# A small copy moved ahead of two others on ScalarE, and twenty unread products near the end

## The chip, the cores and the metric

The kernel runs on one core of a Trainium2 chip. A core has five engines that run side by side, each with a queue of instructions of its own: TensorE (PE in the profile, its weight loads PEld), VectorE (DVE), ScalarE (ACT), GpSimd (POOL) and SyncE (SP), which here only issues DMA transfers. TensorE writes its results to PSUM, which is divided into banks (a tile of 512 float32 numbers per partition fills one here); the other engines carry them from there to SBUF. The metric is the device time of one execution in microseconds. The time before is 2628.5 us, the median of three runs (2627.23 to 2629.38).

## The reference

Two cross-attention layers follow one another on 64 sequences of 256 positions and 320 channels (20 heads of 16). Each sequence has 77 context rows of 512. Cut to what is computed:

```
# layer 0 (the last four of 81 context rows would be image rows; with 77 there are none)
out_text = softmax(q k^T / 4) v              # per head, over 77 context rows
x = x + (out_text) Wo + bo

# layer 1: the first 73 rows are text, the last 4 are image tokens
probs_t  = softmax(q k_t^T / 4)              # over 73
text_out = probs_t v_t
qsem     = l2norm(probs_t text)              # 512 wide, per head and position
sem      = qsem . l2norm(image)^T            # 4 numbers
probs_ip = softmax(q k_ip^T / 4 + 0.5 sem) * spatial_mask
ip_out   = probs_ip v_ip
out      = x + (text_out + ip_out) W_out + b_out
```

All of it is float32.

## The kernel before, in words

x is kept transposed, channels on partitions. Sequences are worked on in pairs: 32 pairs, with index p. A pair has 10 units: two sequences (b), and five units (u) of each, where a unit is 128 positions by 8 heads (the last unit of five takes both halves of the positions for 4 heads). One loop, over g, does one step per unit of layer 0, and beside it one unit of layer 1 that lies 13 steps back. `k = g % 10` is the place of a step in its round of ten; k = 8 is the ninth step, and its successor k = 9 the tenth. After the 320 steps of layer 0 the loop goes on for 25 more, in which layer 1 ends.

A step issues this, in the order of the program:

1. TensorE writes one PSUM tile `sc` of four banks. First come the *semantics* of the layer-1 unit of two steps before (`before1`): its transposed weights times a stored matrix that holds, side by side, the products of the context rows with each other, the values, and ones (lines 755 and 761). Then come the scores of the unit of layer 0 and of the unit of layer 1 (line 641). There is one such tile (`bufs=1`), so these writes wait until all readers of the step before are done.
2. VectorE takes the maximum of the scores (659) and subtracts it (661), for each layer.
3. `transposed(1, ...)`: TensorE transposes the layer-1 weights of the step before (705, 706) and ScalarE copies them out (712, 713). These are read by the next step's 755 and 761.
4. ScalarE computes the exponential for layer 0 (669).
5. `weighted`: VectorE multiplies the first 73 columns of the semantics, in `sc`, by the weights (772, 775), for the norm of `qsem`.
6. `first`: other work of the pipeline, listed by `fillers(k, p)`. In the ninth step these are one or two chunks of value rows: TensorE products (379), and a ScalarE copy (380).
7. `transposed(0, ...)`: the layer-0 weights of the step before, on TensorE (705, 706) and ScalarE (731, 732; 720 and 723 for the fifth unit). Their readers are 788 and 793, in `attend`, after the second and the fifth unit of a sequence.
8. The sums copy (1114): ScalarE copies the other 21 columns of the semantics for 8 heads, 168 numbers per partition, from `sc` to SBUF: four similarities to image tokens, 16 sums of values and the sum of the weights. VectorE's products of point 5 and this copy read the same banks and are kept in order by a wait on VectorE.
9. ScalarE computes the exponentials for layer 1 (672, 673); GpSimd copies the image scores (676).
10. VectorE and GpSimd normalise layer 0 (687, 688, 692), VectorE reduces the products of point 5 (1125).
11. `second` and `third`: more of `fillers`. The last products with image weights (`image_attend_last`, 947) stand here in the ninth step, and the output projection of layer 1 (`project`, 528 and 537, then `project_last`, 616) begins in the tenth.

The order on TensorE, ScalarE, VectorE and GpSimd is the order of the program, held by `keep_order`. SyncE's DMA issues are ordered by a scheduler from the second round on, so an edit elsewhere can shift them.

In the steps after the 320, TensorE has less to do, and `keep_busy(n)` issues n products of the identity with itself into a tile that nobody reads (741). In the very last steps the path is: image weights transposed (914) and copied (916), image outputs (926), VectorE's addition of them (934), the last third of them (947, 951), the output projection (528, 537, 601, 616, 620) and the transfers out.

Of the kernel before, what the change touches and what calls it, by code (L numbers as in the profile page):

```python
# [21 lines left out]
TT = T - NIP  # L22
# [12 lines left out]
UNITS = ((0, 0), (0, 1), (1, 0), (1, 1), (2, 0))  # L35
# [3 lines left out]
NU = 2 * len(UNITS)  # L39
# [24 lines left out]
def tile_two_cross_attentions(ctx: ExitStack, tc: tile.TileContext, a: dict, out: bass.AP):  # L64
# [35 lines left out]
    nc = tc.nc  # L100
    x_in, c_in, cip_in = a["x"], a["ctx"], a["ctx_ip"]
    NB = x_in.shape[1] // S
    NP = NB // 2
# [104 lines left out]
    def load_more(g):  # L208
        queue = nc.sync
        if g == 1:  # L210
            queue.dma_start(cip, cip_in.rearrange("(k p) t -> p k t", p=P))
            load_ctx_weight("wkip1", queue, wkip)
        elif g == 3:
            load_ctx_weight("wvip1", queue, wvip)
        elif g == 5:
            wo[0], bo[0] = load_out("wo0", queue), load_bias("bo0", queue)
        elif g == 6:
            wq[1] = load_chan("wq1", queue)
        elif g == 8:
            wo[1], bo[1] = load_out("wo1", queue), load_bias("bo1", queue)  # L220
            queue.dma_start(smask, a["smask"])
# [404 lines left out]
    stats = {}  # L626
    ws, pts = {}, {}

    def eight(t, u):

        return t[:, PLACES[u] : PLACES[u] + 8].rearrange("p (r e) ... -> p r e ...", e=2)
# [14 lines left out]
    def shifted(ps, l, p, b, u):  # L646


        nt = (T, TT)[l]
        name = f"{l}_{p}_{b}{u}"  # L650
        if l and u == 0:
            stats[p, b] = (
                small.tile([P, 2 * H, NIP], F32, tag="att", name=f"att{p}_{b}", bufs=3),
                big.tile([P, 2 * H, NIP + D + 1], F32, tag="sums", name=f"sums{p}_{b}", bufs=3),
                small.tile([P, 2 * H], F32, tag="nrm", name=f"nrm{p}_{b}", bufs=3),
            )
        sc = ps[:, :, 2 * T * l : 2 * T * (l + 1)].rearrange("p r (e t) -> p r e t", t=T)
        mx = small.tile([P, 4, 2], F32, tag="mx", name=f"mx{name}")
        nc.vector.tensor_reduce(mx, sc[:, :, :, :nt], AX.X, ALU.max)  # L659
        w = ws[l] = sp.tile([P, 4, 2, T], F32, tag=f"w{l}", name=f"w{name}", bufs=2 - l)  # L660
        nc.vector.tensor_tensor(  # L661
            w, sc, mx.unsqueeze(3).broadcast_to([P, 4, 2, T]), ALU.subtract
        )

    def exponential(l, g, p, b, u):

        w = ws[l]
        if not l:
            nc.scalar.activation(w, w, AF.Exp, scale=SCALE)  # L669
            return  # L670
        two = ws[l] = parts1[g % 3]
        nc.scalar.activation(two[:, :4].rearrange("p (e a) j t -> p (a j) e t", e=2), w[:, :, :, :M], AF.Exp, scale=SCALE)  # L672
        nc.scalar.activation(  # L673
            rests(two), w[:, :, :, M:TT], AF.Exp, scale=SCALE
        )
        nc.gpsimd.tensor_copy(eight(stats[p, b][0], u), w[:, :, :, TT:])  # L676

    def rests(two):

        r = two[:, 4].rearrange("p j (a c) -> p (j a) c", c=QR)  # L680
        return r[:, :, : 2 * R1].rearrange("p r (e t) -> p r e t", e=2)
# [52 lines left out]
    def keep_busy(n):  # L734


        if n:
            ps = ptr.tile([P, 4, P], F32, tag="tr", name=f"busy{len(busy)}")
            busy.append(n)
            for i in range(n):  # L740
                nc.tensor.transpose(ps[:, i % 4, :], ident, ident)
# [24 lines left out]
    def by_block(ps):  # L766
        return ps[:, :, SEM0 : SEM0 + 2 * GV].rearrange("p r (e t) -> p r e t", t=GV)

    def weighted(ps, p, b, u, w):
        sm = by_block(ps)  # L770
        prod = sp.tile([P, 4, 2, TT], F32, tag="prod", name=f"prod{p}_{b}{u}", bufs=1)
        nc.vector.tensor_tensor(  # L772
            prod[:, :, :, :M], sm[:, :, :, :M], w[:, :4].rearrange("p (e a) j t -> p (a j) e t", e=2), ALU.mult
        )
        nc.vector.tensor_tensor(prod[:, :, :, M:], sm[:, :, :, M:TT], rests(w), ALU.mult)  # L775
        return prod
# [40 lines left out]
    def text_output(p, b):  # L817

        sums = stats[p, b][1]
        rec = small.tile([P, 2 * H], F32, tag="rec", name=f"rec{p}_{b}", bufs=2)  # L820
        nc.vector.reciprocal(rec, sums[:, :, NIP + D])
        an = big.tile([P, 2, H, D], F32, tag="an", name=f"an{p}_{b}", bufs=1)
        by_head(an, sums[:, :, NIP : NIP + D], rec)
        return an
# [36 lines left out]
    def image_least(p, b):  # L861


        total = stats[p, b][1][:, :, NIP + D]
        t = least[p, b] = small.tile([P, 2 * H], F32, tag="least", name=f"least{p}_{b}", bufs=1)
        nc.gpsimd.tensor_mul(t, total, total)

    def image_squares(p, b):
        r = stats[p, b][2]
        nc.vector.scalar_tensor_tensor(r, least[p, b], EPS * EPS, r, ALU.mult, ALU.max)  # L870
# [181 lines left out]
    def unit(g):  # L1052
        return (g // NU, g % NU // len(UNITS), g % len(UNITS)) if 0 <= g < NP * NU else None
# [6 lines left out]
    for fn in held.pop("q")():  # L1060
        fn()

    last0 = last1 = before1 = None
    later, early = {}, {}
    for g in range(NP * NU + LAG + 12):
        p, k = divmod(g, NU)
        first, second, third, begin = fillers(k, p)
        if g == NU + 3:
            in_order = len(nc.cur_bb.bb.instructions)
        load_more(g)  # L1070
        now = [unit(g), unit(g - LAG)]
        ps = prod = None
        for fn, args in early.pop(g, ()):
            fn(*args)
        drains = [fn for what in ("q", "o") if what in held for fn in held.pop(what)()]
        if now[0] or now[1] or before1:
            ps = psc.tile([P, 4, 512], F32, tag="sc", name=f"sc{g}")
            todo = []
            if before1:
                todo.append((semantics, (*before1[:3], before1[4])))  # L1080
            for l in range(2):
                if now[l]:
                    todo.append((scores, (l, *now[l])))
            for n, (fn, args) in enumerate(todo):
                fn(ps, n == 0, n == len(todo) - 1, *args)
        for fn, args in begin:
            fn(*args)
        if "i" in held:
            drains += held.pop("i")()
        for fn in drains:  # L1090
            fn()
        for l in range(2):
            if now[l]:
                shifted(ps, l, *now[l])
        new1 = None
        if last1:
            transposed(1, *last1)
            new1 = (*last1, pts[1])
        if now[0] and k != 5:
            exponential(0, g, *now[0])  # L1100
        if before1:
            prod = weighted(ps, *before1[:4])
        for fn, args in first:
            fn(*args)
        if last0:
            transposed(0, *last0)
        idle = g - NP * NU
        if idle > 2:
            keep_busy(14 if now[1] else {13: 12, 14: 16, 15: 14, 16: 16, 17: 16}.get(idle, 0))
        if now[0] and k == 5:  # L1110
            exponential(0, g, *now[0])
        ends = before1 and before1[2] == len(UNITS) - 1
        if before1:
            nc.scalar.copy(eight(stats[before1[:2]][1], before1[2]), by_block(ps)[:, :, :, TT:])  # L1114
            if ends:
                image_least(*before1[:2])
        if now[1]:
            exponential(1, g, *now[1])
        for fn, args in later.pop(g, ()):
            fn(*args)  # L1120
        if now[0]:
            normalize(g)
        if before1:
            q, b, u = before1[:3]
            nc.vector.tensor_reduce(eight(stats[q, b][2], u), prod, AX.X, ALU.add)  # L1125
            if ends:
                image_squares(q, b)
                made["an"] = text_output(q, b)
                later[g + 1] = [(image_scores, (q, b))]
                early[g + 2] = [(image_shifted, (q, b)), (image_exponential, (q, b))]  # L1130
                early[g + 3] = [(image_weights, (q, b))]
        for fn, args in second:
            fn(*args)
        if last0:
            q, b, u, _ = last0
            if u == 1 or u == len(UNITS) - 1:
                attend(q, b, int(u > 1))
        for fn, args in third:
            fn(*args)
        if ends:  # L1140
            image_norm(*before1[:2])
        last0 = (*now[0], ws[0]) if now[0] else None
        before1 = new1
        last1 = (*now[1], ws[1]) if now[1] else None
# [51 lines left out]
```

## Time and profile before

| | |
|---|---|
| Median of three runs | 2628.5 us (2627.23 to 2629.38) |
| The profiled execution's own time | 2627.7 us |
| Its span, first to last instruction | 2626.0 us |
| Mean granted TensorE clock | 0.996 |
| Sums copy, line 1114 | 320 times, 302 ns each |
| VectorE's wait that ends the idle time before it | 119.0 us (189 times) |
| Copy of transposes, line 731 | 256 times, 588 ns each |
| Unread products, line 741 | 214 records, 2536.3 to 2607.7 us |

The profile is of one execution. A group row gives source line, engine, operation, the tile written and those read, the count; then busy time in us and mean ns of one; then the engine's idle time just before these instructions and what ended it. A row of the timeline or the chain has start, duration, engine and line. In a row for a stretch of time, the granted clock (1.00 is full speed) stands after the busy times, and then the share of the DMA engines and their GB/s. L705 is line 705.

### The profile page before, as it was taken

The page shows a single profiled execution, that of the slowest core. Times are in us where ns is not written, and L with a number is a line of the kernel's source. Part 1 is how long each engine was busy: PE and PEld are TensorE (multiplying, and loading weights), DVE is VectorE, ACT ScalarE, POOL GpSimd, SP SyncE. Part 2 cuts the span into 40 slices and gives each one's busy share as a digit, 9 for nine tenths or more (in the row PEclk, how much of TensorE's full clock was granted, in tenths as well). Part 3 has the DMA queues.
Part 4 walks back from the last instruction along what each step waited for, and adds up shares of the span by engine and source line. Part 5 has one row for each costly group of instructions (what it writes and reads, how often), then busy time and mean ns, then how long its engine had stood idle before and what let it go on. Part 6 is the DMA issues. An engine that isn't in the chain of part 4 may idle for free.

```text
span 2626.0 us, 74027 instructions
## 1 busy us (share of the span) xinstructions
PE 2558.2 (97%) x27006; PEld 1981.0 (75%) x27006; DVE 1972.3 (75%) x3641; ACT 1539.2 (59%) x3989; POOL 1440.1 (55%) x3514
## 2 busy tenths in 40 slices
PE   7999999999999999999999999999999999999998
PEld 5677777777777777777777777777777777777676
DVE  3577777777777777777777777777777777777764
ACT  3465665665665665665665665665665665665553
POOL 2455555565555566555566555566555556555542
PEclk9999999999999999999999999999999999999999
DMA  5212211112111112211112111112211112211000
GB/s 163 72 29 58 58 42 47 42 51 57 51 50 47 43 51 56 58 43 47 42 52 57 51 50 47 42 52 57 56 46 47 42 52 56 55 41 36 26 22 23
DMA packets 154657, 132.26 MB, mean 50 GB/s; under 512 B 48248, under 2 KB 132984, under 8 KB 154296
## 3 DMA queue, kind: packets, MB, share of 16 engines
q1 hardware_dynamic: 153432, 126.38, 17.9%
q8 instruction: 216, 3.54, 0.6%
q14 instruction: 145, 1.19, 0.2%
q10 hardware_dynamic: 864, 1.15, 0.1%
HBM read 89.53 MB, written 33.91 MB: 47 GB/s over the span
## 4 chain that ended last, share of the span: by engine, by line
PE 85%; DVE 7%; ACT 3%; DMA 2%; issue 1%; POOL 1%; SPq 1%; DVEq 0%; POOLq 0%; ACTq 0%
PE sc L755 12%; PE tr L705 11%; PE o_ps L528 8%; PE sc L641 7%; PE v_ps L379 6%; PE sc L761 4%; PE q_ps L528 4%; PE q_ps L555 4%; PE k_ps L334 4%; PE o_ps L616 3%; PE o_ps L537 3%; PE pv L788 2%; DVE w L661 2%; PE q_ps L563 2%; PE q_ps L557 2%; DVE mx L659 2%
## 5 line engine op out<-in xcount | busy, mean ns | idle before, releaser
L659 DVE TENSOR_REDUCE mx<-sc 128x8 f32<-128x584 f32 (+1 forms) x640 | 497.8, 778 | 461.1 <-PE sc L641 461.1
L692 POOL TENSOR_TENSOR parts<-w,sm 128x512 f32<-128x512 f32 (+1 forms) x640 | 439.7, 708 | 299.8 <-ACT parts L673 180.7
L661 DVE TENSOR_TENSOR w<-sc,mx 128x616 f32<-128x616 f32 x640 | 512.0, 800 | 66.7 <-DVE mx L659 0.5
L712 ACT COPY pt<-tr 128x512 f32<-128x512 f32 x320 | 186.8, 584 | 446.6 <-PE tr L705 435.0
L705 PE MATMUL tr<-ident,parts 128*128 128x128 f32 x2560 | 410.4, 283 | 11.1 <-POOL parts L692 5.3
L755 PEld LDWEIGHTS sc<-gv,pt 64*128 64x128 f32 x5120 | 317.9, 188 | 108.8 <-ACT sums L1114 60.3
L755 PE MATMUL sc<-gv,pt 64*128 64x94 f32 x5120 | 357.6, 279 | 27.9 <-ACT sums L1114 27.7
L705 PEld LDWEIGHTS tr<-ident,parts 128*128 128x128 f32 x2560 | 283.0, 141 | 122.2 <-issue 87.0
L676 POOL COPY att<-w 128x32 f32<-128x32 f32 x320 | 66.8, 209 | 471.9 <-DVE w L661 471.4
L669 ACT ACTIVATE w<-w 128x616 f32<-128x616 f32 x320 | 232.0, 725 | 96.8 <-DVE w L661 96.2
L687 DVE TENSOR_REDUCE sm<-w 128x8 f32<-128x616 f32 x320 | 248.6, 777 | 14.0 <-ACT w L669 14.0
L641 PE MATMUL sc<-kbd,q 32*128 32x154 f32 x5120 | 248.5, 306 | 1.0 <-ACT q L586 0.8
L528 PE MATMUL o_ps<-aT,wo 128*128 128x256 f32 x1024 | 233.4, 381 | 0.0
L1125 DVE TENSOR_REDUCE nrm<-prod 128x8 f32<-128x584 f32 x320 | 227.6, 711 | 0.4
L772 DVE TENSOR_TENSOR prod<-sc,parts 128x512 f32<-128x512 f32 x320 | 218.0, 681 | 4.0 <-PE sc L761 4.0
L528 PEld LDWEIGHTS o_ps<-aT,wo 128*128 128x128 f32 x1024 | 190.7, 191 | 24.0 <-DVE aT L934 0.4
L672 ACT ACTIVATE parts<-w 128x512 f32<-128x512 f32 x320 | 206.8, 646 | 0.0
L641 PEld LDWEIGHTS sc<-kbd,q 32*128 32x128 f32 x5120 | 187.3, 187 | 6.0 <-issue 5.0
L731 ACT COPY pt<-tr 128x512 f32<-128x512 f32 x256 | 150.6, 588 | 67.4 <-PE tr L705 66.7
L379 PE MATMUL v_ps<-wv,cf 128*128 128x320 f32 (+1 forms) x624 | 182.1, 438 | 0.0
L706 PE MATMUL rtr<-ident,parts 128*104 128x128 f32 (+1 forms) x640 | 175.0, 273 | 0.0
L1114 ACT COPY sums<-sc 128x168 f32<-128x168 f32 x320 | 96.6, 302 | 120.2 <-DVE prod L775 119.0
(151 smaller groups left out, 4838.5 us busy)
## 6 DMA issues: line engine op xcount, KB each, us to landing
vip<-vip_rows SPq DMA_DIRECT2D x1280, 5.0 KB
out_dram<-x SPq DMA_DIRECT2D x64, 256.0 KB
x<-in_x_dram SPq DMA_DIRECT2D x31, 512.0 KB
v_rows<-vs SPq DMA_DIRECT2D x38, 320.0 KB
vm<-v_rows SPq DMA_DIRECT2D x152, 80.0 KB
ct<-in_ctx_dram SPq DMA_DIRECT2D x32, 308.0 KB
cf<-in_ctx_dram SPq DMA_DIRECT2D x38, 256.0 KB
g_rest<-gram_rest SPq DMA_DIRECT2D x512, 0.5 KB
```

The lines of the kernel that those rows point to most:

```text
L379: nc.tensor.matmul(ps[:n, :C], cfs[i][:, k, :n], wv[l][:, k, :], start=(k == 0), stop=(k == KE - 1))
L528: nc.tensor.matmul(ps[b][:, m, :], w[:, k, m * P : (m + 1) * P], main[:, k, b * S : (b + 1) * S], start=(k == 0 and m == 0), stop=False,)
L641: nc.tensor.matmul(ps[:, r, 2 * T * l : 2 * T * (l + 1)], q[rows, b, :] if part == 2 else q[rows, t0 : t0 + P], kbd[rows, part].rearrange( ...
L659: nc.vector.tensor_reduce(mx, sc[:, :, :, :nt], AX.X, ALU.max)
L661: nc.vector.tensor_tensor(w, sc, mx.unsqueeze(3).broadcast_to([P, 4, 2, T]), ALU.subtract)
L669: nc.scalar.activation(w, w, AF.Exp, scale=SCALE)
L687: nc.vector.tensor_reduce(sm, w, AX.X, ALU.add)
L692: nc.gpsimd.tensor_tensor(two[:, 8 * t0 : 8 * t1].rearrange("p (h t) -> p h t", h=8), w[:, :, t0:t1], sm.unsqueeze(2).broadcast_to([P, 8, ...
L705: nc.tensor.transpose(ps[:, i, :], flat[:, i * P : (i + 1) * P], ident)
L755: nc.tensor.matmul(ps[:, i % 2 * 2 + j, at : at + GV], pt[half_rows, i, :], gv[b][half_rows, part, i, :], start=start and i < 2, stop=False,)
L772: nc.vector.tensor_tensor(prod[:, :, :, :M], sm[:, :, :, :M], w[:, :4].rearrange("p (e a) j t -> p (a j) e t", e=2), ALU.mult)
L1125: nc.vector.tensor_reduce(eight(stats[q, b][2], u), prod, AX.X, ALU.add)
```

## The change

Two things change.

The sums copy becomes a function `sums_out`, which is called in one of two places. In the ninth step of a round it is called after `first` and before `transposed(0, ...)`, so that ScalarE's queue holds it ahead of the two copies of the transposes (731, 732). In the other nine steps it stays where it was. `ends`, which tells whether the unit is the last of its sequence, is computed earlier, since the function reads it.

In the last steps, 20 more unread products are issued: eight between the transposes of the last image weights (914) and the last image outputs (926), for which the transposes are taken out of `second` and issued first; six between 926 and 947; and six between 947 and the last projection (528).

```diff
+    def sums_out(ps):
+        nc.scalar.copy(eight(stats[before1[:2]][1], before1[2]), by_block(ps)[:, :, :, TT:])
+        if ends:
+            image_least(*before1[:2])
+
...
+        ends = before1 and before1[2] == len(UNITS) - 1
         for l in range(2):
             if now[l]:
                 shifted(ps, l, *now[l])
...
             prod = weighted(ps, *before1[:4])
+        if g - NP * NU in (18, 19):
+            keep_busy(6)
         for fn, args in first:
             fn(*args)
+        if before1 and k == 8:
+            sums_out(ps)
         if last0:
             transposed(0, *last0)
         idle = g - NP * NU
         if idle > 2:
             keep_busy(14 if now[1] else {13: 12, 14: 16, 15: 14, 16: 16, 17: 16}.get(idle, 0))
+        if idle == 17:
+            fn, args = second.pop(0)
+            fn(*args)
+            keep_busy(8)
         if now[0] and k == 5:
             exponential(0, g, *now[0])
-        ends = before1 and before1[2] == len(UNITS) - 1
-        if before1:
-            nc.scalar.copy(eight(stats[before1[:2]][1], before1[2]), by_block(ps)[:, :, :, TT:])
-            if ends:
-                image_least(*before1[:2])
+        if before1 and k != 8:
+            sums_out(ps)
         if now[1]:
             exponential(1, g, *now[1])
```

## The prediction

> **What bounds the kernel now.** First the page: the busy shares and the share of the chain by engine. Its group rows then name what ends TensorE's idle time.
>
> ```profile
> PE 2558.2 (97%) x27006; PEld 1981.0 (75%) x27006; DVE 1972.3 (75%) x3641; ACT 1539.2 (59%) x3989; POOL 1440.1 (55%) x3514
> PE 85%; DVE 7%; ACT 3%; DMA 2%; issue 1%; POOL 1%; SPq 1%; DVEq 0%; POOLq 0%; ACTq 0%
> L755 PE MATMUL sc<-gv,pt 64*128 64x94 f32 x5120 | 357.6, 279 | 27.9 <-ACT sums L1114 27.7
> L1114 ACT COPY sums<-sc 128x168 f32<-128x168 f32 x320 | 96.6, 302 | 120.2 <-DVE prod L775 119.0
> ```
>
> TensorE is busy for 97% and is 85% of the chain, so only a change in its own work or in its idle time counts. The largest idle time that one wait ends is 27.7 us ahead of L755, the first products of a step, which write the banks that the sums copy L1114 reads. I went through the 320 first products of L755 by place in the round of ten. Two places of ten wait in every round. In the seventh step it is 0.32 to 0.33 us, behind a sums copy that itself waits for the vector engine's L775. In the tenth it is 0.349 to 0.351 us in 29 rounds, 0.38 in the last full one and 1.10 in the first. The change touches the second of these. The chain there, one of the 29:
>
> ```profile
> 1241.64 0.42 ACT vs L380
> 1242.07 0.01 issue
> 1242.08 0.59 ACT pt L731
> 1242.67 0.17 ACT pr L732
> 1242.83 0.21 ACT sums L1114
> 1243.04 0.04 issue
> 1243.08 1.13 PE sc L755 x16
> ```
>
> For 1.4 us the chain leaves TensorE and runs over ScalarE's queue. The two copies between L380 and L1114 are what the change moves behind L1114. The timeline there says what else could hold L755:
>
> ```profile
> 1241.56 0.22 DVE L775 TENSOR_TENSOR prod<-sc,parts 128x72 f32<-128x72 f32 x1
> 1242.08 0.65 PE L947 MATMUL ipv<-iwT,vip 80*64 80x256 f32 x4
> 1242.72 0.31 ACT L1114 COPY sums<-sc 128x168 f32<-128x168 f32 x1
> 1243.08 1.13 PE L755 MATMUL sc<-gv,pt 64*128 64x94 f32 x16 [0.35 <-ACT sums L1114]
> 1243.45 0.28 ACT L673 ACTIVATE parts<-w 128x72 f32<-128x72 f32 x1
> 1245.11 0.66 PE L705 MATMUL tr<-ident,parts 128*128 128x128 f32 x4
> 1245.24 0.80 DVE L659 TENSOR_REDUCE mx<-sc 128x8 f32<-128x616 f32 x1 [1.56 <-PE sc L641]
> 1245.86 0.58 ACT L712 COPY pt<-tr 128x512 f32<-128x512 f32 x1 [2.13 <-PE tr L705]
> ```
>
> L775, for which L1114 has to wait, is done at 1241.78. TensorE's own work L947 ends at 1242.73.
>
> For the end of the kernel, the clock by stretch (busy times per engine, then PEclk) and the timeline:
>
> ```profile
> 2606.28:2609.69 3.41, 2.62 (x21) 1.00 0.00 0
> 2609.69:2613.10 3.41, 3.07 (x14) 1.00 0.00 0
> 2613.10:2616.52 3.42, 3.42 (x10) 0.50 0.00 0
> ```
>
> ```profile
> 2611.84 0.86 PE L947 MATMUL ipv<-iwT,vip 80*64 80x256 f32 x4 [0.34 <-DVE aT L934]
> 2612.63 5.41 PE L528 MATMUL o_ps<-aT,wo 128*128 128x256 f32 x16
> ```
>
> The granted clock is half for 3.41 us just as the last large products L528 begin.
>
> **The change part by part.** *The sums copy ahead of the two copies, ninth step.* The built program has it straight behind L380 on ScalarE, 31 times. Usual round: L380 ends at 1242.06. Neighbouring copies there overlap by about 0.13 us (L732 begins at 1242.56, L731 ends at 1242.67), so the sums copy runs from about 1241.95 to 1242.25, and L755 could follow 0.05 us later, as now (1243.03 to 1243.08): at 1242.30. TensorE is then not ready: L947 ends at 1242.73. Where L755 follows L947 without a wait (2569.30, behind an L947 that ends at 2569.36), it begins 0.07 us before that end. So it begins at 1242.66 and gains 0.42 us, the 0.35 of idle time and 0.07 of overlap. Done for every round with its own times, this gives 0.42 in each of the 29, together 12.2 us. In the round around 2187 L775 ends only 0.57 us ahead of the old sums copy, and 0.16 us is left to spare. In the first round (L775 ends at 137.64, ScalarE is free at 137.1) and the last (2502.94 against 2502.3) the copy is held by L775, not by the copies ahead of it: 0.02 us is lost in each. The sum is 12.1 us. Bounds: 29 x 0.349 = 10.1 if the overlap isn't had, 12.2 at most, since TensorE has no more idle time there.
>
> *What stands behind the moved copy.* L731 and L732 end some 0.1 to 0.2 us later. Their weights are of the unit that is third of five, and the products that read them (L788, L793) come only two steps on. Their transpose buffers are written next by L705 at 1245.11, 2 us later. The exponentials L672 and L673 follow the same three copies as before and keep their time. Even 0.86 us late, as in the first and last rounds, L673 would end at 1244.6, ahead of L705 (1245.11, or 1244.69 when that moves up). The copy makes nothing wait on GpSimd: no least-sums product is issued in the ninth step. The tenth step follows TensorE: its first reduction waits 1.56 us for TensorE's scores and its first copy 2.13 us for the transposes. So the later sums copy at 1250.44, which has only 0.09 us in hand before the next L755, moves up with it.
>
> *SyncE.* Its order shifts a little in most rounds: one 5 KB row of image values goes behind the gram's transfers and later ones, and the gram's go one issue (0.36 us) earlier. Cost nothing. The rows that move late are issued from 1350.26 on, and GpSimd multiplies the next set only after 1409. The set that is nearer (20 rows, 1323.53 to 1330.74, product L480 at 1331.95) keeps its place. Should L480 wait by the 0.42 us that TensorE gains, GpSimd stands idle 0.50 us behind it, which covers that; uncovered it would be 12 us.
>
> *The 20 products at the end.* The trace has such products 0.109 us apart, the first 0.165 ahead of the second, and about 0.2 from the last to another kind. Eight after the image transposes: they run from about 2608.7 to 2609.6, so that L926 begins at 2609.7 instead of 2609.53: 0.2 us late. Six after L926: L947 waits for L934 and would come at 2612.04; the six let it begin at 2612.35, 0.5 late in all. Six ahead of L528, with nothing to wait for: 1.1 us late in all. Against that, L528 took 5.34 us to L537 at the half clock, and 3.55 at the full one (2446.13 to 2449.68). If the products keep the clock up, 1.8 is saved and 0.7 is left. Bounds: all 20 on the path, 20 x 0.109 = 2.2 us lost; all hidden and the clock kept, 1.8 gained. I take the gain of 0.7: the stretches from 2602.9 to 2609.7 hold hardly anything but these products and transposes, at PEclk 1.00, while the stretch ahead of the drop holds L926 and L947, on 32 and 80 of 128 partitions, and 1 us of idle time.
>
> [...]
>
> *Sum.* 12.1 + 0.7 = 12.8. The profiled execution took 2627.7 (span 2626.0 and 1.7 around it) and would take 2614.9. The median shown, 2628.5, is 0.8 above it: **2615.7**.
>
> **The rivals.** *The products cost and the clock drops all the same* (or, in an execution whose stretches lie otherwise, it would not have dropped before): 12.1 gained, 1.1 lost, 2617.5. For it: the clock's stretches needn't lie at the same places in each execution. Against it: the full clock up to 2613.1 above. [...]
>
> *The gain is given back in the tenth step,* because the next sums copy doesn't move up: only its 0.09 us in hand stays, 29 x 0.09 = 2.6, with the 0.7: 2625.2. Against it: that copy's chain begins at TensorE's L641 and L705, as the two waits show.
>
> *The change doesn't do what it says:* L755 is released by something else that ends at 1243.03, and only the end gains: 2627.8. Against it: in all 31 rounds L755 of the tenth step begins 0.05 us behind the end of L1114.
>
> *Slower.* The sums copy now stands ahead of the two copies in ScalarE's queue and waits for L775. If L775 ends later than in the trace, ScalarE stands and L755 with it. It decides from L755 at 1243.08: the copy must begin 0.78 us later than 1241.95 for no gain, and 0.18 more per round (5.3 / 29) for a loss that can be told, so L775 would have to end 1.1 us later than it does. At 1.3 us: 29 x 0.4 = 11.6 lost, 2640. For it: the first and last rounds have that order of ends. Against it: in the 29 L775 ends 0.57 to 3.1 us ahead of the old copy, the same from round to round.
>
> **How the numbers follow.** Two tenths of a percent, 5.3 us, is about what a measurement of this kernel can tell from no change. Chances: the forecast 0.72, products that only cost 0.15, given back 0.04, nothing done 0.04, slower 0.05. So faster 0.87, same 0.08, slower 0.05. The range holds the first two: from 2628.5 - 12.2 - 1.8 - 1.3 (the fastest run below the median) = 2613.2 to 2628.5 - 10.1 + 2.2 + 0.9 (the slowest above it) = 2621.5.
>
> **What would show it.** After: L755 in the tenth step with no idle time and 0.42 us closer to L947; the sums copy straight behind L380, about 0.4 us ahead of L947's end; L755's wait for sums down from 27.7 to about 17.5 us, some 10 of them in the seventh step; the span from 29 rounds of 77.8 to 83.2 us, each shorter by 0.42; PEclk 1.00 through L528 near the end, L926 0.2, L947 0.5 and L528 1.1 us later against L914. Wrong it would be by a new wait ahead of L705 or L755 in the tenth and first steps, by L1114 waiting for L775 in the middle rounds, or by half-clock stretches elsewhere: the one from 2473.15 to 2483.40 could cost or save up to 5 us.

## The result, and the profile after

The median fell from 2627.86 us (6 runs, 2624.44 to 2630.64) to 2615.70 us (6 runs, 2612.19 to 2619.86). The ratio is 0.9954, with a 95% interval from 0.9941 to 0.9967: about 12 us less, 8.7 to 15.5 by the interval. The predicted time was 2615.7. The profiled execution after took 2612.19 us (span 2610.4, mean granted clock 0.998), against 2627.7 (span 2626.0, clock 0.996) before. It is the fastest of its six, so the two profiles lie 15.5 us apart where the medians lie 12.2 apart. The working below has to say which part of that is the change.

The page of the kernel after: busy time by engine, the shares of the chain, and the two groups that the change is about. In it the first products of a step are still L755, and the sums copy is L1064.

```profile
PE 2552.0 (98%) x27026; PEld 1979.1 (76%) x27026; DVE 1971.3 (76%) x3641; ACT 1535.6 (59%) x3989; POOL 1439.9 (55%) x3514
...
PE 84%; DVE 7%; DMA 3%; ACT 2%; POOL 1%; issue 1%; SPq 1%; DVEq 0%; POOLq 0%; ACTq 0%
...
L755 PE MATMUL sc<-gv,pt 64*128 64x94 f32 x5120 | 356.3, 278 | 17.4 <-ACT sums L1064 17.2
...
L1064 ACT COPY sums<-sc 128x168 f32<-128x168 f32 x320 | 96.4, 301 | 122.5 <-DVE prod L775 121.3
```

TensorE's wait for the sums copy fell from 27.7 to 17.2 us. ScalarE went from 3% to 2% of the chain. The copy itself is as long as before (301 ns) and waits about as long for VectorE (121.3 us, 119.0 before): nothing became faster, something only stands elsewhere. The chain in the tenth step of the round that the prediction showed (start, duration, what):

```profile
1235.47 0.54 PE v_ps L379 x2
1236.01 0.44 PE tr L705 x4
1236.45 0.11 PE rtr L706
1236.56 0.58 PE ipv L947 x4
1237.14 1.06 PE sc L755 x16
```

Before, the chain left TensorE there for 1.4 us. Now it stays on it. The timeline of the same place (start, duration, engine, line, and in brackets idle time and what ended it):

```profile
1235.96 0.22 DVE L775 TENSOR_TENSOR prod<-sc,parts 128x72 f32<-128x72 f32 x1
...
1236.05 0.43 ACT L380 COPY vs<-v_ps 128x320 f32<-128x320 f32 x1 [0.76 <-PE v_ps L379]
...
1236.37 0.30 ACT L1064 COPY sums<-sc 128x168 f32<-128x168 f32 x1
...
1236.49 0.65 PE L947 MATMUL ipv<-iwT,vip 80*64 80x256 f32 x4
1236.56 0.61 ACT L731 COPY pt<-tr 128x512 f32<-128x512 f32 x1
...
1237.07 1.13 PE L755 MATMUL sc<-gv,pt 64*128 64x94 f32 x16
...
1239.23 0.80 DVE L659 TENSOR_REDUCE mx<-sc 128x8 f32<-128x616 f32 x1 [1.15 <-PE sc L641]
```

The sums copy stands straight behind L380 and ends at 1236.67. L755 has no bracket any more: it begins 0.40 us after the copy's end, and 0.07 us ahead of the end of L947 (1237.14), so TensorE is now what it waits for. L731 and L732 end 0.10 and 0.09 us later behind L380 than before. The reduction L659 waits 1.15 us where it waited 1.56: the next step came forward by those 0.41 us.

I went through all 31 rounds. L755 has no idle time in 29 of them, and each of the 29 rounds is 0.42 us shorter. The first and the last round keep theirs (1.10 and 0.36 us).

The end of the kernel on TensorE after:

```profile
2593.10 1.06 PE L914 MATMUL itr<-ident,iw 128*80 128x128 f32 x4
2594.00 1.04 PE L741 MATMUL busy<-ident 128*128 128x128 f32 x8
2594.97 1.88 PE L926 MATMUL ipv<-iwT,vip 32*128 32x256 f32 x8
2596.77 0.87 PE L741 MATMUL busy<-ident 128*128 128x128 f32 x6
2597.58 0.65 PE L947 MATMUL ipv<-iwT,vip 80*64 80x256 f32 x4
2598.16 0.87 PE L741 MATMUL busy<-ident 128*128 128x128 f32 x6
2598.87 3.62 PE L528 MATMUL o_ps<-aT,wo 128*128 128x256 f32 x16
2602.42 1.13 PE L537 MATMUL o_ps<-aT,wo 64*128 64x256 f32 x8
```

And the same place by stretches (busy time of TensorE first, then the other engines; the number after them is the granted clock):

```profile
2595.40:2598.80 3.40, 3.40 (x24) 2.22 (x23) 1.71 (x3) 0.00 (x0) 0.00 (x0) 1.00 0.03 5
2598.80:2602.20 3.40, 3.40 (x19) 2.93 (x16) 0.00 (x0) 0.00 (x0) 0.00 (x0) 1.00 0.00 0
```

The clock is full through L528. Counted from the first L914, in us:

| | L926 | L947 | L528 | L537 | last instruction |
|---|---|---|---|---|---|
| before | 1.74 | 4.06 | 4.84 | 10.18 | 18.20 |
| after | 1.86 | 4.47 | 5.77 | 9.32 | 17.35 |

The products hold L528 up by 0.93 us, L528 itself is 1.79 us shorter, and 0.86 us is gained.

**The 15.5 us between the two profiles, by place.** The 29 rounds give 29 x 0.42 = 12.2. The end gives 0.9. A half-clock stretch of before (2473.16 to 2483.4, in the last full round) is missing after, which is worth 3.4. Smaller differences at the start, half-clock stretches among them, come to about 0.5. And five steps in the middle lose 1.7 together. That makes 15.3 of the 15.5. The 3.4 and most of the -1.7 aren't shown to be of the change: seven other profiles with the moved copy have half clock in the last full round from about the same place, and steps behind late rows lose as much with the copy in its old place. In the six executions after, the span grows as the clock falls, and the one with the trace has the highest clock:

| | | | | | | |
|---|---|---|---|---|---|---|
| span, us | 2610.4 | 2612.0 | 2613.0 | 2614.9 | 2615.9 | 2618.1 |
| mean granted clock | 0.998 | 0.997 | 0.996 | 0.996 | 0.995 | 0.994 |

The missing stretch, as before had it (of which the first row is what stands ahead of the drop):

```profile
2469.70:2473.15 3.45, 1.34 (x12) 1.09 (x10) 3.24 (x6) 2.27 (x8) 0.94 (x2) 1.00 0.18 49
2473.15:2476.60 3.45, 3.30 (x36) 3.13 (x40) 2.13 (x5) 3.40 (x6) 2.89 (x7) 0.50 0.00 0
2476.60:2480.00 3.40, 2.85 (x18) 1.95 (x14) 2.67 (x4) 1.15 (x4) 0.49 (x1) 0.50 0.00 0
```

TensorE is busy for 1.34 of 3.45 us, in the idle time ahead of an L755 of the last round, and then runs at half clock for three stretches. And the middle steps that lose, here the largest, after:

```profile
1989.14 0.72 POOL L453 TENSOR_TENSOR v<-vm,half 128x320 f32<-128x320 f32 x1 [3.09 <-DMA v_rest<-v_rows]
1990.76 0.70 POOL L365 TENSOR_TENSOR kbd<-kT,head_mask 128x308 f32<-128x308 f32 x1
...
1991.49 0.28 ACT L337 COPY kT<-k_ps 128x146 f32<-128x146 f32 x1 [2.01 <-POOL kbd L365]
1991.83 0.51 PEld L528 LDWEIGHTS q_ps<-x,wq 128*128 128x128 f32 x3 [1.36 <-ACT kT L337]
1991.83 0.70 PE L528 MATMUL q_ps<-x,wq 128*128 128x256 f32 x2 [0.95 <-ACT kT L337]
```

GpSimd's L453 waits 3.09 us for value rows, L365 stands behind it on that engine, L337 waits for L365, and TensorE for L337. The waits of before have 0.4 us of TensorE ahead of L528, behind L337; those of after have 1.6. One of the five steps has another cause:

```profile
1657.16 0.80 DVE L661 TENSOR_TENSOR w<-sc,mx 128x616 f32<-128x616 f32 x1 [0.46 <-DVE mx L659]
...
1660.75 1.13 PE L557 MATMUL q_ps<-x,wq 128*128 128x256 f32 x4 [0.35 <-DVE x L620]
```

VectorE stands for 0.46 us between its own L659 and L661, its later work comes some 0.35 us later for it, and TensorE's L557 waits 0.35 us for VectorE's L620. The profile before has such a pause too (0.47 us), but at 2183.00, where TensorE loses nothing by it. Among the kernels run here with the whole move of the copy, nine of eleven have the pause at 1656 to 1660 and the 0.35 us ahead of L557, and two have neither. The kernel before and the two runs with the copy in its old place or half way have the pause at 2182 to 2183, and L557 doesn't wait. So these 0.35 us go with the change in nearly all of its profiles. Why VectorE pauses is open.

### The profile page after: what moved, and what is told of

The parts are those of the page before. It is cut to its first block, busy times and chain, and to the rows that moved or that the text cites. A ratio compares the mean times of both kernels' runs of the same rounds, so it can differ in the third digit from the quotient of the medians.

```text
span 2610.4 us, 74097 instructions
## 1 busy us (share of the span) xinstructions
PE 2552.0 (98%) x27026; PEld 1979.1 (76%) x27026; DVE 1971.3 (76%) x3641; ACT 1535.6 (59%) x3989; POOL 1439.9 (55%) x3514
## 3 DMA queue, kind: packets, MB, share of 16 engines
q10 hardware_dynamic: 864, 1.15, 0.1%
## 4 chain that ended last, share of the span: by engine, by line
PE 84%; DVE 7%; DMA 3%; ACT 2%; POOL 1%; issue 1%; SPq 1%; DVEq 0%; POOLq 0%; ACTq 0%
PE sc L755 12%; PE tr L705 11%; PE o_ps L528 8%; PE sc L641 7%; PE v_ps L379 6%; PE sc L761 4%; PE q_ps L528 4%; PE q_ps L555 4%; PE k_ps L334 3%; PE o_ps L616 3%; DVE w L661 3%; PE pv L788 2%; PE o_ps L537 2%; DVE mx L659 2%; PE q_ps L557 2%; PE rtr L706 2%
## 5 line engine op out<-in xcount | busy, mean ns | idle before, releaser
L659 DVE TENSOR_REDUCE mx<-sc 128x8 f32<-128x584 f32 (+1 forms) x640 | 497.3, 777 | 446.9 <-PE sc L641 446.8
L661 DVE TENSOR_TENSOR w<-sc,mx 128x616 f32<-128x616 f32 x640 | 511.8, 800 | 67.0 <-ACT w L669 0.5
L755 PEld LDWEIGHTS sc<-gv,pt 64*128 64x128 f32 x5120 | 316.9, 187 | 96.0 <-ACT sums L1064 47.3
L755 PE MATMUL sc<-gv,pt 64*128 64x94 f32 x5120 | 356.3, 278 | 17.4 <-ACT sums L1064 17.2
L528 PE MATMUL o_ps<-aT,wo 128*128 128x256 f32 x1024 | 231.6, 379 | 0.0
L528 PEld LDWEIGHTS o_ps<-aT,wo 128*128 128x128 f32 x1024 | 189.7, 190 | 23.0
L672 ACT ACTIVATE parts<-w 128x512 f32<-128x512 f32 x320 | 207.1, 647 | 0.0
L731 ACT COPY pt<-tr 128x512 f32<-128x512 f32 x256 | 151.1, 590 | 67.1 <-PE tr L705 66.8
L1064 ACT COPY sums<-sc 128x168 f32<-128x168 f32 x320 | 96.4, 301 | 122.5 <-DVE prod L775 121.3
```

Of the source, the lines that this page charges most:

```text
L528: nc.tensor.matmul(ps[b][:, m, :], w[:, k, m * P : (m + 1) * P], main[:, k, b * S : (b + 1) * S], start=(k == 0 and m == 0), stop=False,)
L661: nc.vector.tensor_tensor(w, sc, mx.unsqueeze(3).broadcast_to([P, 4, 2, T]), ALU.subtract)
L755: nc.tensor.matmul(ps[:, i % 2 * 2 + j, at : at + GV], pt[half_rows, i, :], gv[b][half_rows, part, i, :], start=start and i < 2, stop=False,)
```

## The experiments

Ratios are to the kernel before on the same chip, with 95% intervals.

**The moved copy alone.** The first experiment keeps the copy's new place and takes out the 20 products.

```diff
-        if g - NP * NU in (18, 19):
-            keep_busy(6)
...
-        if idle == 17:
-            fn, args = second.pop(0)
-            fn(*args)
-            keep_busy(8)
```

> The sums copy goes ahead of the two copies in the ninth step; the 20 more products at the end are left out. Theory (ScalarE's order held L755): L755 of the tenth step has no idle time ahead of it in 29 rounds, 29 x 0.42 = 12.2 us, less some 1.2 to 1.7 us in a few rounds where a load for GpSimd comes late, so 10.5 to 11 us below the kernel before, whatever the clock does near the end. Rival (the end of the kernel gave a large part of the 12.2 us that were measured): no more than 8 us below.

Measured: 2616.1 us (5 runs, 2611.95 to 2618.01) against 2626.79; ratio 0.9956 (0.9943 to 0.9968). L755's waits are those of after. The end is that of before: L528 4.83 and the last instruction 18.19 us after L914. By stretches:

```profile
2598.05:2601.50 3.45, 2.81 (x13) 1.59 (x13) 1.29 (x2) 0.24 (x1) 0.00 (x0) 1.00 0.00 0
2601.50:2604.95 3.45, 3.45 (x9) 2.75 (x9) 0.42 (x1) 0.00 (x0) 0.00 (x0) 0.51 0.02 5
```

The clock is half among L528 again, although the drop could have lain elsewhere in another execution. There is half clock from 2465.0 to 2471.8 as well, the stretch that was missing in the profile of after: the moved copy doesn't remove it. The copy gives 10.7 us by the medians, nearly all there is, and the drop at L528 is back without the products.

**The 20 products alone.**

```diff
-        if before1 and k == 8:
-            sums_out(ps)
...
-        if before1 and k != 8:
+        if before1:
             sums_out(ps)
```

> The 20 products alone; the sums copy stays behind the two copies in every step. Theory (the products keep the granted clock up): the steps as in the kernel before, L755 of the tenth step 0.35 us idle; near the end L926 0.13, L947 0.43 and L528 0.93 us later against L914, the clock at 1.00 through L528, so that L528 takes 3.55 us to L537: 0.9 us less than where the clock had dropped there, 0.9 more in an execution in which it had not. Rival (such products don't count for the clock): half clock for 3.41 us among L528, 0.9 us slower in every execution.

Measured: 2626.28 us (11 runs); ratio 0.9993 (0.9984 to 1.0002). L755 waits 0.35 us in the tenth step as before. The end is that of after, row by row (1.86, 4.47, 5.77, 9.32, 17.35), with the clock at 1.00 through L528. The medians give 0.5 us, which the interval does not tell from nothing; the rows give 0.86. One more thing is in this profile: TensorE waits 1.7 us ahead of L528 at 2000.2, behind late value rows, without the moved copy. So those waits do not need it.

**The copy between the two others.** If its place in ScalarE's queue sets L755, half the way should give half the gain.

```diff
+    between = []
...
         nc.scalar.copy(pt[:, :, s * P : (s + 1) * P], ps)
+        while between:
+            between.pop()()
         nc.scalar.copy(rt[:, s * P : (s + 1) * P], pr[:n, 0, :])
...
         if before1 and k == 8:
-            sums_out(ps)
+            if last0:
+                between.append(lambda ps=ps: sums_out(ps))
+            else:
+                sums_out(ps)
```

> As the changed kernel, but in the ninth step the sums copy stands between the two copies: behind the large one (L731), ahead of the small one (L732). Theory (the place in ScalarE's queue sets when L755 begins): the sums copy ends about 0.15 us earlier than in the kernel before, L755 of the tenth step is left with 0.17 to 0.20 us of idle time, and 0.15 to 0.18 x 29 = 4.4 to 5.2 us of the gain are had instead of 12.2; the whole about 7 us above the changed kernel. Rival (something else releases L755, or it is enough that L732 follows): no idle time and the changed kernel's time.

Measured: 2621.99 us (11 runs); ratio 0.9984 (0.9975 to 0.9993). The timeline in the tenth step (lines are shifted here: L758 is L755, L1067 the sums copy, L732 and L735 the two copies):

```profile
1242.17 0.43 ACT L380 COPY vs<-v_ps 128x320 f32<-128x320 f32 x1 [0.75 <-PE v_ps L379]
1242.60 0.59 ACT L732 COPY pt<-tr 128x512 f32<-128x512 f32 x1
...
1243.09 0.30 ACT L1067 COPY sums<-sc 128x168 f32<-128x168 f32 x1
1243.28 0.28 ACT L735 COPY pr<-rtr 104x128 f32<-104x128 f32 x1
...
1243.44 1.13 PE L758 MATMUL sc<-gv,pt 64*128 64x94 f32 x16 [0.18 <-ACT sums L1067]
```

L758 waits 0.18 us in each of the 29 rounds. That is 0.17 less than before, which is what the short copy took in the chain, and 0.25 more than after, where it overlaps L947 by 0.07. 29 x 0.17 = 4.9 us. The medians give 4.8 against the kernel before and 4.3 against the kernel with the products alone, which this one has too. The wait follows the place in the queue.

**The products that the copy waits for, twice.** How far is L775 from being next? This kernel computes them twice in the ninth step, which adds some 0.9 us on VectorE.

```diff
         if before1:
+            if k == 8:
+                weighted(ps, *before1[:4])
             prod = weighted(ps, *before1[:4])
```

> As the changed kernel, but VectorE's two products (L772, L775) are computed twice in the ninth step, 0.83 to 0.9 us more for it; the second writes the same numbers. Theory (L775 is the next one behind the copies): L775 now ends at or a little after the time at which the copies of the kernel before were done; the sums copy waits for it some 0.5 to 0.7 us, L755 of the tenth step is again 0.3 to 0.45 us idle, and the gain of the middle rounds is gone: 10 to 13 us above the changed kernel. Rival (another wait would have come first, or VectorE's time has room of more than 0.9 us): L755 without idle time, the changed kernel's time.

Measured: 2627.8 us (11 runs); ratio 1.0004 (0.9995 to 1.0013), 12.1 us above the changed kernel.

```profile
1242.47 0.43 ACT L380 COPY vs<-v_ps 128x320 f32<-128x320 f32 x1 [0.75 <-PE v_ps L379]
...
1243.25 0.22 DVE L775 TENSOR_TENSOR prod<-sc,parts 128x72 f32<-128x72 f32 x1
1243.51 0.30 ACT L1064 COPY sums<-sc 128x168 f32<-128x168 f32 x1 [0.61 <-DVE prod L775]
...
1243.86 0.91 PE L755 MATMUL sc<-gv,pt 64*128 64x94 f32 x12 [0.30 <-ACT sums L1064]
```

With L775 0.86 us later, the copy waits 0.61 us for it here, and L755 waits for the copy in 23 of the 29 rounds, 0.30 us in nearly all of them, and 1.97 and 1.22 in the first and the last. In the other six rounds, in which L775 of the kernel before ends 3.09 us ahead of the copy instead of some 0.9, nothing is lost. By the rows that makes 8.7 us in the 29 rounds and 1.7 in the first and the last, 10.4 above the changed kernel of the 12.2 that were gained; the rest of the 12.1 between the medians lies within the spread of the executions. In 23 rounds L775 is the next thing in line.

**One transfer for the image rows.** The late value rows might come from SyncE's issues. This kernel puts one transfer for 80 partitions in place of 20 rows each.

```diff
-        for h in range(H):
-            nc.sync.dma_start(vip[h * NIP : (h + 1) * NIP, :], vip_rows[r0 : r0 + NIP, :])
+        nc.sync.dma_start(vip, vip_rows[r0 : r0 + NIP, :].unsqueeze(0).broadcast_to([H, NIP, C]))
```

> As the changed kernel, but the 20 rows of image values of a sequence are brought by one transfer of 80 partitions from a repeated source instead of 20 transfers, which takes 19 x 64 issues of some 0.36 us from SyncE. In four of six profiles so far TensorE stood 0.3 to 1.7 us more in a few middle rounds (502, 815, 1660, 1992), ahead of L528 and L557, behind GpSimd's L453, which waited 2 to 3 us for value rows. Theory (SyncE's issues are what makes these rows late): L453 waits for no transfer in the middle rounds, L528 and L557 have no idle time there, 1 to 2 us less than the changed kernel. Rival (they are late for another reason, the transfers themselves or what SyncE waits for): the waits of L453 stay.

Measured: 2618.06 us (5 runs); ratio 0.9964 (0.9950 to 0.9977). L453 still waits 2.26, 2.27, 2.37 and 2.62 us for value rows, and L528 still 1.0 us in all. The theory fell: the 20 issues of the image rows are not the cause. L557 has no idle time here, but VectorE doesn't pause here either; the expectation put that step behind L453, which is not what it waits for. The end gained something that the expectation didn't name: L926 takes 1.13 us instead of 1.88, and the last instruction ends 16.65 us after L914 instead of 17.35. Only this edit has it among all the traces; why was not looked into, and the median doesn't show it. This profile has half clock from 2462.3 to 2472.6, too.

**The same in the seventh step.** There 0.32 us is left ahead of L755 in every round, behind a copy that waits 0.48 us for L775. Here, in the step that issues that copy, VectorE's products are issued ahead of layer 1's part of `shifted`, so that L775 ends earlier.

```diff
             if now[l]:
                 shifted(ps, l, *now[l])
+            if not l and before1 and k == 5 and now[0]:
+                prod = weighted(ps, *before1[:4])
...
-        if before1:
+        if before1 and prod is None:
             prod = weighted(ps, *before1[:4])
```

> As the changed kernel, and in the sixth step VectorE computes the two products (L772, L775) ahead of layer 1's maximum and subtraction instead of behind them. Theory (the other wait of a round, L755 of the seventh step, hangs on L775 through the sums copy): L775 ends some 1.5 us earlier, the sums copy follows L669 at once, L755 of the seventh step has no idle time, 0.32 + 0.07 = 0.39 us in 30 rounds, 11.7 us less than the changed kernel, about 2604. Rival (layer 1's subtraction, which now comes 0.9 us later, makes the exponentials and with them L705 late, or VectorE becomes the bound, since its idle time ahead of the next maximum is only 0.49 us): the gain is halved or gone.

Measured: 2611.91 us (5 runs, 2611.59 to 2612.5); ratio 0.9941 (0.9928 to 0.9953). The median is lower, but not for the reason that was expected:

```profile
1213.35 0.22 DVE L775 TENSOR_TENSOR prod<-sc,parts 128x72 f32<-128x72 f32 x1
...
1214.37 0.80 DVE L661 TENSOR_TENSOR w<-sc,mx 128x616 f32<-128x616 f32 x1
1215.21 0.30 ACT L1064 COPY sums<-sc 128x168 f32<-128x168 f32 x1 [0.48 <-DVE w L661]
...
1215.56 1.13 PE L755 MATMUL sc<-gv,pt 64*128 64x94 f32 x16 [0.32 <-ACT sums L1064]
```

L775 is done 1.6 us ahead, and the copy now waits just as long, 0.48 us, for L661, the last access of VectorE to the same banks that was issued ahead of it. L755 still waits 0.32. The span (2610.2) is that of after (2610.4). What sets this kernel apart is that all five executions are near 2612. Their mean clocks are 0.997 and 0.998, and the half clock of the last full round is missing in this profile, as in that of after. Why this order should keep the clock up is open.

**The copy ahead of layer 1's `shifted` as well.** If L661 is the last one, the copy has to be issued ahead of it.

```diff
+        soon = k == 5 and before1 and now[0] and now[1]
         for l in range(2):
-            if now[l]:
+            if now[l] and not (l and soon):
                 shifted(ps, l, *now[l])
+        if soon:
+            prod = weighted(ps, *before1[:4])
...
-        if before1:
+        if before1 and not soon:
             prod = weighted(ps, *before1[:4])
...
-        if before1 and k == 8:
+        if before1 and (k == 8 or soon):
             sums_out(ps)
+        if soon:
+            shifted(ps, 1, *now[1])
...
-        if before1 and k != 8:
+        if before1 and k != 8 and not soon:
             sums_out(ps)
```

> As the changed kernel; in the sixth step VectorE computes the products ahead of layer 1's maximum, and the sums copy is issued between them, behind ScalarE's L713 and the step's other copy and ahead of L720 and L723, so that layer 1's maximum waits for the copy and no longer the copy for layer 1's subtraction. Theory (what held the copy in the run before was the last reader of its banks that was issued ahead of it): the copy ends some 1.6 us earlier, L755 of the seventh step has no idle time, 0.39 us in 30 rounds, 11.7 us less than the changed kernel. Rival (VectorE, 0.5 us later, becomes the bound in the seventh step, where it has 0.49 us of idle time): half of it is given back, 5 to 6 us less.

Measured: 2618.49 us (6 runs); ratio 0.9969 (0.9958 to 0.9981), no gain.

```profile
1216.60 0.30 ACT L1064 COPY sums<-sc 128x168 f32<-128x168 f32 x1 [0.40 <-DVE prod L775]
1216.93 0.77 DVE L659 TENSOR_REDUCE mx<-sc 128x8 f32<-128x584 f32 x1 [0.36 <-ACT sums L1064]
1217.80 0.80 DVE L661 TENSOR_TENSOR w<-sc,mx 128x616 f32<-128x616 f32 x1
...
1218.65 1.13 PE L755 MATMUL sc<-gv,pt 64*128 64x94 f32 x16 [0.28 <-DVE w L661]
```

Now VectorE stands 0.36 us for the copy, and L755 waits for VectorE's L661 itself. Each round became 0.10 us longer, 30 x 0.1 = 3 us. In this step VectorE's own accesses to the banks end last, and the order of the copy did not help; the theory fell.

**Without any products near the end.** Do the unread products hold the clock at all? This kernel leaves out the 20, as the first experiment does, and also the 32 of the two steps before them. None of them is read.

```diff
-        if g - NP * NU in (18, 19):
-            keep_busy(6)
...
-            keep_busy(14 if now[1] else {13: 12, 14: 16, 15: 14, 16: 16, 17: 16}.get(idle, 0))
+            keep_busy(14 if now[1] else {13: 12, 14: 16, 15: 14}.get(idle, 0))
...
-            keep_busy(8)
```

> As the changed kernel, but without the 20 products and without the 32 unread products of the two steps ahead of them (those that stood ahead of the image transposes L914). Theory (unread products count for the granted clock): the clock drops to half earlier than in the kernel before, ahead of L914 or L926, and stays down for 6.8 us or more, so that L926 to L528 take longer, 2 to 4 us in all from the last attention outputs to the end. Rival (they don't count): the clock as in the kernel before, half for 3.41 us from about the start of L528.

Measured in one execution: 2615.76 us. By stretches:

```profile
2590.07:2593.49 3.42, 1.19 (x8) 0.47 (x5) 0.72 (x2) 2.02 (x7) 1.95 (x4) 1.00 0.00 0
2593.49:2596.90 3.41, 0.93 (x3) 0.35 (x3) 0.72 (x2) 0.80 (x2) 1.01 (x4) 0.50 0.00 0
2596.90:2600.30 3.40, 3.04 (x11) 2.22 (x12) 1.29 (x2) 0.00 (x0) 0.00 (x0) 0.50 0.00 0
2600.30:2603.75 3.45, 3.45 (x11) 2.26 (x8) 0.42 (x1) 0.00 (x0) 0.00 (x0) 0.50 0.00 0
```

The clock is half for 10.2 us, three times as long as before, from behind the first stretch that lacks the products. L926 takes 2.50 us instead of 1.88, L947 1.34 instead of 0.65, and L528 5.0 us to L537 instead of 3.55. The products do hold the clock up. All the profiles agree with it: in the eleven of kernels with 14 or 20 of them the clock is full from L914 to L537, and in the three without (before, the moved copy alone, this one) it drops there. In this profile no L528 in the middle waits over 0.15 us for L337, though the order there is that of after and L453 waits 2.0 to 2.2 us: that loss differs from one execution to the next. The 0.35 us ahead of L557 is here too.

**Fourteen instead of twenty.** Left out are the six ahead of L528.

```diff
-        if g - NP * NU in (18, 19):
+        if g - NP * NU == 18:
             keep_busy(6)
```

> As the changed kernel, but without the last six products, those ahead of L528. Theory (they alone delay L528, and the clock is held up by the fourteen): L528 begins 0.55 to 0.65 us earlier against L914, at about 5.15 to 5.2, the clock at 1.00 through L528. Rival (the six are needed): half clock for 3.41 us among L528, 1.8 us longer to L537.

Measured in one execution: 2615.46 us. L528 begins 5.03 us after the first L914 instead of 5.77, the clock stays 1.00 through it, and the last instruction ends at 16.71 instead of 17.35. The six are not needed for the clock here, and cost 0.64 us.

**Filling the idle time of the last round.** With the fourteen, 12 products go into the idle time ahead of L755 where before dropped to half clock.

```diff
-        if g - NP * NU in (18, 19):
+        if g - NP * NU == 18:
             keep_busy(6)
...
         idle = g - NP * NU
+        if idle == -6:
+            keep_busy(12)
```

> As the changed kernel, but the six products ahead of L528 are left out (0.63 us less in the profile without them), and 12 unread products stand at the end of the step in the last round in which TensorE is otherwise idle for 2.26 us (in front of 2462). In nine of ten profiles so far the clock was half for 6.8 to 10.2 us behind that idle time; in the changed kernel's profile it was not. Theory (the spread of the changed kernel, 2612 to 2620, is that drop, which some executions have and some not, and products would hold the clock there too): no half clock between 200 and 2600 us, all executions within about 1 us of 2611.5. Rival (the spread has another cause): a spread of 5 us and more, median 2615.

Measured: 2615.44 us (5 runs, 2611.84 to 2616.86); ratio 0.9952 (0.9940 to 0.9964). Its profile has full clock from 152 us to 2609.7, at the end. But the executions still spread over 5 us, at mean clocks from 0.995 to 0.999. So that stretch was at full clock here, which the profile of after shows without such products too, and the spread has other sources as well; which, is open, since only one execution of each kernel has a trace. Of the ten profiles that the expectation counts, eight had the drop and not nine: that of the kernel with VectorE's products ahead of layer 1's `shifted` lacks it too.

**The last two together,** that is this filling and the copy ahead of layer 1's `shifted`.

> The changes of the two runs above together. Theory: their gains add up, since the one lies in 30 middle rounds and the other near the end: about 2600 us, within 1 us from execution to execution. Rival: the half of the first, 2606.

Measured: 2615.64 us (5 runs); ratio 0.9955 (0.9943 to 0.9968). The 0.10 us per round is lost here too, and there is half clock again from 2484.8 to 2488.2.

**The best parts.** The products ahead of layer 1's `shifted`, whose five executions were the lowest, with the fourteen:

```diff
+            if not l and before1 and k == 5 and now[0]:
+                prod = weighted(ps, *before1[:4])
...
-        if before1:
+        if before1 and prod is None:
...
-        if g - NP * NU in (18, 19):
+        if g - NP * NU == 18:
```

> The order of the kernel with the products ahead of the second shift, and fourteen unread products at the end instead of twenty (the six ahead of L528 left out, which cost 0.64 us in the profile of the kernel with fourteen). Theory A, what an execution takes goes by the granted clock, and which stretches fall to half differs by execution and not by this edit: the median is 2613.5 to 2616 again, the executions spread over 4 us or more, and the five executions near 2611.9 of the kernel with twenty were chance. Theory B, this order itself keeps the clock up in the last full round: all executions lie within 1.5 us and the median is 2610.8 to 2611.8, with no stretch at half between 2440 and 2600. Both expect L755 of the seventh step 0.32 idle behind a sums copy that waits 0.48 for L661, and L528 begun 4.9 to 5.1 us after the first L914 at PEclk 1.00.

Measured: 2612.45 us (5 runs, 2612.06 to 2615.94); ratio 0.9951 (0.9938 to 0.9965). L755 of the seventh step waits 0.32 us, and L528 begins 5.04 us after L914 at full clock, as both theories had it. Half clock is back between 2463 and 2469 in the profile, and the executions spread over 3.9 us, so theory B fell. The median is 1 us below what theory A gave, which leaves open whether this order helps the clock in some executions. Both intervals, this one's and that of the kernel with twenty products in the same order, overlap that of the changed kernel, so neither of the two is shown to beat it.

## Why the prediction was right, step by step

*The copy ahead of the transposes' copies: right, and shown.* The 29 rounds gained 0.42 us each, the 0.35 of idle time and the 0.07 of overlap. The kernel with the copy alone has it, the one with the products alone has not, the one with the copy half way has 0.17 of it. The first and last rounds, put at a loss of 0.02 each, lost nothing (1.10 and 0.36 us against 1.10 and 0.38).

*What stands behind the copy: right.* L731 and L732 came 0.10 and 0.09 us later (0.1 to 0.2 predicted), L672 and L673 kept their distance to L380 within 0.14, and the tenth step followed TensorE. The overlap of neighbouring copies, about 0.13 us in the prediction's words, is 0.11 by its own rows, and 0.11 after.

*SyncE's order at no cost: not refuted, but the rows named were not those that came late.* L480 did not hold TensorE up. Steps behind L453 did, with 1.6 us in the profile after and 0.4 before. The kernel with the products alone waits 1.7 us at one such step without the moved copy, the one with far fewer issues 1.0, and one with the copy moved (the one without any products near the end) hardly at all. So nothing shows these waits as a price of the change; the sum lacked a term for how much such steps vary between executions. Why the rows come 2 to 3 us late is open. The 0.35 us ahead of L557, behind VectorE's pause, is another matter: it stands in nine of the eleven profiles with the whole move and in none of the others, and the sum has no term for it.

*The 20 products: right in direction, mis-sized by 0.2.* L926, L947 and L528 came 0.12, 0.41 and 0.93 us later where 0.2, 0.5 and 1.1 were put, and 1.79 was saved where 1.8 was put: 0.86 instead of 0.7.

*The clock under the unread products: as forecast, and shown.* With the 20 products the clock is 1.00 from L914 to L537, and where products are left out it is half for 3.4 us (20 fewer) or 10.2 us (52 fewer). Had it dropped all the same, the products alone would have cost 1.1 us, as the prediction priced them.

*The sum.* It gave 12.8 off the profile. The changed rows gave 12.2 + 0.86 = 13.0 in the profile, and 12.2 between the medians. That the median is the predicted one to 0.1 us is partly luck: the six executions spread over 7.7 us, and the median shown ahead of the prediction was 0.6 above the later one. Of the things that would make it wrong, the half-clock stretch from 2473.15 was named at up to 5 us; it was absent from the profile after, for 3.4 us, so that profile alone (15.5 us) would have looked better than the change is. The rival in which L775 comes late did not occur, but the kernel with VectorE's products twice shows its mechanism. The prediction put the point of no gain at a copy 0.78 us later. There it begins 0.72 us later (0.61 behind L380's end instead of 0.11 ahead of it), and 0.05 of the 0.35 us is left. That rival counted all 29 rounds at one price, though six of them have some 2 us more in hand, and these lost nothing.

## What to carry to other kernels

Go through a wait by its place in the loop, not by its total. Then ask, for each place, which engine's queue holds the releaser up and what stands next in line: moving a copy ahead of two others paid where only its queue place held it (tenth step, 0.42 us a round), and paid nothing where a reader of the same banks on another engine ended last (seventh step, 0.10 us a round lost). Give a time as small as this a range from the spread of executions, and compare profiles only after taking out the stretches where the clock differs.

## What the runs showed of the hardware

*A busier stretch was followed by half clock, and less busy ones were not.* In before, a stretch with TensorE busy for 3.07 of 3.41 us, with L926 on 32 partitions and L947 on 80, was followed by half clock; with 14 products among them (the kernel with fourteen) it was not, and the clock stayed 1.00 through L528. The stretch ahead of it, busy for only 2.62 us, was followed by full clock, and so was one behind it (2619.93 to 2623.34, with L616 on 128 partitions), busy for 1.51. So in these rows idle time alone does not decide. What does is not shown.

*The same kernel's executions spread by 1 to 9 us of some 2620, and the mean granted clock goes with it* (in the six after, 0.998 at a span of 2610.4 to 0.994 at 2618.1). Single profiled executions lay between 3.6 us below the median of their kernel and 2.3 above it.

*In the seventh step the sums copy waited for the access of VectorE to its banks that was issued last ahead of it,* whichever columns that one reads: 0.48 us for L775 in one order, 0.48 for L661 in the other, where L775 had been done for 1.6 us. This is how the waits of these two programs run; that the banks themselves enforce it wasn't tried.
